# Short GpSimd memsets between the gathers of a two-layer graph network

## The chip, the cores and the metric

The kernel runs on one core of a Trainium2 chip. The core has five engines that work side by side[...]: PE (matrix products), DVE (vector work), ACT (activations), POOL (GpSimd, which here mostly issues gathers) and SP (which here only issues DMAs). The metric is the device time of one execution in microseconds (us), as the median of several executions.

## The reference

There are N = 6250 nodes with 256 features and 200,000 edges with 128 attributes. The edges are sorted by their destination `dst`; their sources `src` are random. Two layers follow one another, each with a residual and a layer norm.

```python
# layer 1: messages over the edges, added up by destination
e = edge_attr @ W_edge + b_edge
msg = relu(x[src] + e)
agg = segment_sum(msg, dst)
h = (1 + eps) * x + agg
h = relu(h @ W1 + b1) @ W2 + b2
h = relu(batchnorm_over_nodes(h) * gamma + beta)
x = layernorm(x + h)
# layer 2: attention with 4 heads of 64
z = einsum('nd,hdf->nhf', x, W)
e = leaky_relu(es[src] + ed[dst])      # es, ed: products of z with att
alpha = softmax of e over the edges of one destination
out = segment_sum(alpha * z[src], dst)
x = layernorm(x + out)
```

Both layers read one row of a table for each edge at random: `x[src]` in the first, `z[src]` in the second. Those are the gathers that this case is about.

## The kernel before

**Tiles.** The edges are cut into 1563 subtiles of 128 edges (one edge to a partition), and 14 subtiles make a group (`S = 14`), so there are 112 groups, the last with 9 subtiles. Since the edges are sorted, the destinations of a group lie in a window of at most 128 neighbouring nodes, and one-hot matrices on PE do the segment sums.

**Layer 1** (`edge_messages`) works through pairs of subtiles. For pair k:

- `fetch` (L537, gathers at L542) issues on POOL one indirect DMA for each subtile, which reads 128 rows of 256 floats by the ids in a column of `src_sb` into half of a tile `XG[k]`. The pool of these tiles holds 14 pairs, so POOL can be up to 28 gathers ahead of their use. The first 20 groups read the input x, later ones a table `xb_tab` with the bias added in.
- `features` (L546) computes the edge term on PE into PSUM.
- `sums` (L554, L556) adds the gathered rows on DVE; with this the tile `XG[k]` comes free.
- `upper` (ACT, L561) and `lower` (DVE, L565) take the relu as the sum of a high and a low part, and `add_up` (PE, L575) adds both up by destination into an accumulator of the group.

When a group ends, `flush` (L454) corrects the accumulator, runs the two dense layers of the window and keeps statistics for the batch norm.

**The middle** (`middle`, L677) takes the batch norm, layer norm and the tables of layer 2; POOL adds the residual there (L727).

**Layer 2** works by groups. `gather` (L877, gathers at L883) issues on POOL 14 gathers of 264 floats from `z_tab` into a ring of 4 groups. DVE computes the weights and multiplies the rows by them (`weigh`, y at L1007), PE adds them up (L1011), and `leave` finishes the rows of a group (`finish_steps`: fin at L369, the layer norm's root by way of L322 and L325) and sends them out.

**What sets the order.** The bodies of both layers stand in a block which fixes the order of four engines as written:

```python
with tc.manual_schedule(engines={ET.DVE, ET.PE, ET.Activation, ET.SP}):
```

POOL is not among them. Its instructions are put in order by the scheduler of the language, which keeps what data and buffers demand and is otherwise free to choose. The same holds in layer 2 (L1047).

Of the kernel before, what the change touches and what calls it, by code (L numbers as in the profile page):

```python
# [6 lines left out]
F32 = mybir.dt.float32  # L7
# [25 lines left out]
XB_FROM = 20  # L33
RING = 4
XTB = 4
FIRST = 256
IN_RANGE = "the value is an id of a node, which the kinds of inputs bound"

# [10 lines left out]
def gnn(ctx, tc, io, N, E):  # L49
    nc = tc.nc  # L50
# [10 lines left out]
    def groups(g):  # L61
        return range(gs[g], gs[g + 1])
# [4 lines left out]
    const = ctx.enter_context(tc.tile_pool(name="const", bufs=1))  # L67
# [40 lines left out]
    nc.vector.memset(nil, 0.0)  # L108
    ones3 = const.tile([3, P], BF16, name="ones3")
    nc.vector.memset(ones3, 1.0)  # L110


    gf = const.tile([P, 2 * G], F32, name="gf")
# [325 lines left out]
    with ExitStack() as st:  # L439
# [97 lines left out]
        def fetch(k):  # L537
            g, j0, w = pairs_[k]
            XG[k] = gp.tile([P, 2, D], F32, tag="xg", name="xg")
            for i in range(w):  # L540
                t = gs[g] + j0 + i
                nc.gpsimd.indirect_dma_start(  # L542
                    out=XG[k][:, i, :], out_offset=None, in_=io["x"] if g < GB else xb_tab,
                    in_offset=bass.IndirectOffsetOnAxis(ap=src_sb[:, t:t + 1], axis=0))

        def features(k):  # L546
            g, j0, w = pairs_[k]
            pt = PT[k] = pe.tile([P, 2, D], F32, tag="pe", name="pt")
            for i in range(w):
                if g < GB:  # L550
                    nc.tensor.matmul(pt[:, i, :], ones3, bias3, start=True, stop=False)
                nc.tensor.matmul(pt[:, i, :], EA.pop(gs[g] + j0 + i), we_sb, start=not g < GB, stop=True)  # L552
# [35 lines left out]
        with tc.manual_schedule(engines={ET.DVE, ET.PE, ET.Activation, ET.SP}):  # L588
# [16 lines left out]
            for f in (0, 1):  # L605
                if f < K:
                    fetch(f)
                    features(f)
# [8 lines left out]
            for k in range(K + 2):  # L617
# [10 lines left out]
                j = k - firsts_[g] if k < K else 99  # L628
                if k + 2 < K:
                    fetch(k + 2)  # L630
                    features(k + 2)
# [45 lines left out]
    def middle(h2T, stats):  # L677

        with ExitStack() as st:
# [28 lines left out]
            nc.sync.dma_start(ed_tab[NB * P:], zero[:, 0, :EW])  # L708
            cuts = [0] + [min(c0, NB * P) for c0 in range(FIRST, NB * P + CH, CH)]
            cs = list(zip(cuts, cuts[1:]))  # L710
            M = {}

            def load(ci):
                c0, c1 = cs[ci]
                xt = yp.tile([P, 2, CH], F32, tag="xt", name="xt", bufs=XTB)
                nc.sync.dma_start(xt[:, :, :c1 - c0], io["xT"].rearrange("(k p) n -> p k n", p=P)[:, :, c0:c1])
                M["xt", ci] = xt
# [75 lines left out]
            none = iter(())  # L793
            for ci in range(min(XTB - 1, nch)):
                load(ci)
            with tc.manual_schedule(engines={ET.DVE, ET.PE, ET.Activation, ET.SP}):
                for i in range(nch + 3):
                    if i + XTB - 1 < nch:
                        load(i + XTB - 1)
                    a, b, d = (f(j) if 0 <= j < nch else none  # L800
# [45 lines left out]
    with ExitStack() as st:  # L846
# [20 lines left out]
        def size(g):  # L867
            return gs[g + 1] - gs[g]
# [8 lines left out]
        def gather(g):  # L877
            n = size(g)
            slot = T["slot"] if T["slot"] + n <= RING * S else 0
            T["slot"] = slot + n  # L880
            zg = ring[:, slot:slot + n]
            for j, t in enumerate(groups(g)):
                nc.gpsimd.indirect_dma_start(  # L883
                    out=zg[:, j, :], out_offset=None, in_=z_tab,
                    in_offset=bass.IndirectOffsetOnAxis(ap=src_sb[:, t:t + 1], axis=0))
            T["zg", g] = zg

        def loads(g):
# [157 lines left out]

        with tc.manual_schedule(engines={ET.DVE, ET.PE, ET.Activation, ET.SP}):  # L1047
            gather(0)
            loads(0)
            loads(min(1, G - 1))  # L1050
# [4 lines left out]
            for i in range(G + 2):  # L1055
# [3 lines left out]
                if i + 1 < G:  # L1059
                    gather(i + 1)  # L1060
# [253 lines left out]
```

## Time and profile before

| what | value |
|---|---|
| median of 3 runs | 5119.02 us (5110.36 to 5121.45) |
| the profiled execution's own time | 5185.35 us |
| its span on the core | 5183.5 us |
| layer 1's gathers (L542) | 1563, some 0.95 us busy each |
| layer 2's gathers (L883) | 1563, 0.960 us busy each |
| POOL busy | 3014.6 us, 58% of the span |
| mean granted clock of PE | 0.775 |

Layer 1 takes roughly the first 2560 us, the middle some 125 us, and layer 2 runs from about 2685 to 5110 us, with a tail to the end of the span.

How to read it: the profile gives for each engine the busy time and the number of instructions. In a row of a group, the name after the line and engine is what the instruction writes and, after the arrow, reads; behind the bar stand its total busy time, the mean of one in ns, and the time that the engine idled just before such instructions with what ended the idling (the releaser). "issue" as a releaser means that nothing which the profile shows was waited for, and "remote" that the wait ended by an event that the profile can't put down to one of the instructions. A row of waits reads: engine and line that waited, what it waited for, us in total, times, and the longest. A row of windows gives a stretch, its length, busy time and number of the chosen instructions, and then granted clock, DMA share and GB/s.

### The profile page before, as it was taken

What the parts mean: (1) busy time and instruction counts of PE and PEld (TensorE: products, weight loads), DVE (VectorE), ACT (ScalarE), POOL (GpSimd) and SP (SyncE); (2) the same over time, 40 slices, a digit from 0 to 9 for tenths busy, and PEclk for the clock granted to TensorE, in tenths of its full rate; (3) what the DMA queues carried; (4) which work ended last, traced back from release to release, by engine and by line L of the source; (5) the groups of instructions that cost most, each with busy time, mean ns of one, the idle gap of its engine ahead of it and who ended that gap; (6) DMA issues with size and microseconds to landing.
All of it is one profiled execution on the core that took longest, in us unless ns stands there. A gap on an engine that the chain in (4) does not pass through costs nothing. (4 is left out here: it accounts for less than half of the span.)

```text
span 5183.5 us, 49111 instructions
## 1 busy us (share of the span) xinstructions
PE 3157.2 (61%) x12883; PEld 2163.7 (42%) x12883; DVE 3178.2 (61%) x8203; ACT 1055.2 (20%) x3046; POOL 3014.6 (58%) x3158
## 2 busy tenths in 40 slices
PE   6888666556666666666653655655555655555555
PEld 3455454444545445544542333333333333333333
DVE  4665656555565556655664666666666666666666
ACT  2222222222222222222340111111111111111111
POOL 5565565555555555555446666666666666656662
PEclk9898888888887888888876677666667667767667
DMA  4644443333444443434373444444444444444442
GB/s 157 212 133 132 141 133 115 125 106 127 130 132 130 130 134 125 123 127 132 95 198 107 126 116 126 125 124 118 117 120 122 122 120 120 124 119 120 119 115 70
DMA packets 298029, 656.24 MB, mean 127 GB/s; under 512 B 86827, under 2 KB 170139, under 8 KB 290572
## 3 DMA queue, kind: packets, MB, share of 16 engines
q0 software_dynamic: 150144, 416.54, 29.4%
q1 hardware_dynamic: 146090, 235.43, 13.4%
q8 instruction: 106, 1.74, 0.1%
q14 instruction: 183, 1.50, 0.1%
q10 hardware_dynamic: 1506, 1.04, 0.1%
HBM read 617.82 MB, written 34.99 MB: 126 GB/s over the span
## 5 line engine op out<-in xcount | busy, mean ns | idle before, releaser
L883 POOL DMA_INDIRECT ring<-z_tab,src_sb x1563 | 1500.6, 960 | 944.9 <-DVE frs L325 377.8
L1011 PE MATMUL acc<-y,oh 128*128 128x260 f32 x3126 | 1178.6, 521 | 1013.6 <-DVE y L1007 914.9
L542 POOL DMA_INDIRECT xg<-xb_tab,src_sb x1283 | 1213.1, 946 | 886.7 <-DVE pt L556 537.9
L552 PE MATMUL pt<-we_sb,ea_t 128*128 128x256 f32 x3126 | 1036.4, 453 | 477.6 <-DVE hl L565 410.6
L1011 PEld LDWEIGHTS acc<-y,oh 128*128 128x128 f32 x3126 | 722.7, 252 | 1307.3 <-DVE y L1007 1061.5
L552 PEld LDWEIGHTS pt<-we_sb,ea_t 128*128 128x128 f32 x3126 | 626.3, 222 | 675.1 <-issue 463.4
L556 DVE TENSOR_TENSOR pt<-pt,xg 128x512 f32<-128x512 f32 x782 | 540.9, 692 | 432.6 <-PE acc L575 168.2
L575 PE MATMUL acc<-hl,oh 128*128 128x512 f32 x1563 | 721.8, 546 | 1.1 <-DVE hl L565 1.1
L561 ACT ACTIVATE hl<-pt 128x512 fp32r<-128x512 f32 x782 | 466.3, 597 | 1096.0 <-DVE pt L556 634.3
L1007 DVE TENSOR_TENSOR y<-ring,cst 128x520 f32<-128x520 f32 x782 | 528.4, 676 | 77.9 <-remote 57.9
L565 DVE SCALAR_TENSOR_TENSOR hl<-pt,hl 128x512 fp32r<-128x512 f32 x782 | 532.0, 680 | 2.0 <-ACT hl L561 2.0
L369 DVE SCALAR_TENSOR_TENSOR fin<-rows,edw,fin 128x256 f32<-128x256 f32 x112 | 54.0, 482 | 671.0 <-remote 661.4
L542 POOL DMA_INDIRECT xg<-in_x,src_sb x280 | 266.4, 951 | 191.6 <-DVE pt L556 115.0
L575 PEld LDWEIGHTS acc<-hl,oh 128*128 128x128 f32 x1563 | 341.1, 218 | 62.4 <-DVE hl L565 1.9
L414 DVE SCALAR_TENSOR_TENSOR pmk<-p,mk 128x128 f32<-128x128 f32 x224 | 56.3, 289 | 474.2 <-ACT h2T L404 456.5
L400 PE MATMUL p<-r,w_sb 128*128 128x128 f32 x896 | 152.3, 323 | 256.5 <-ACT r L395 169.7
L400 PEld LDWEIGHTS p<-r,w_sb 128*128 128x128 f32 x896 | 133.3, 225 | 294.8 <-ACT r L395 188.0
L523 DVE TENSOR_TENSOR oh<-iota_p,dloc 128x896 fp32r<-128x896 f32 x224 | 241.3, 1078 | 0.0
L322 ACT ACTIVATE frs<-fmv,eps_c 128x1 f32<-128x1 f32 x112 | 33.0, 295 | 1020.5 <-DVE fmv L373 910.4
L933 DVE TENSOR_TENSOR oh<-cst,dloc 128x896 f32<-128x896 f32 x224 | 239.5, 1069 | 0.2 <-ACT cst L993 0.2
L1023 ACT COPY ag<-acc 128x260 f32<-128x260 f32 x111 | 41.6, 375 | 616.7 <-issue 359.6
L395 ACT ACTIVATE r<-p,cols 128x128 f32<-128x128 f32 x224 | 69.8, 364 | 380.2 <-remote 290.2
(219 smaller groups left out, 2940.9 us busy)
## 6 DMA issues: line engine op xcount, KB each, us to landing
ea_t<-in_eaT SPq DMA_DIRECT2D x54, 1792.0 KB
dlb<-dl_tab SPq DMA_DIRECT2D x111, 448.0 KB
ring<-z_tab,src_sb POOLq DMA_INDIRECT x1563
xg<-xb_tab,src_sb POOLq DMA_INDIRECT x1283
xw<-in_x SPq DMA_DIRECT2D x112, 128.0 KB
hw<-hT_tab SPq DMA_DIRECT2D x112, 128.0 KB
out<-o SPq DMA_DIRECT2D x110, 128.0 KB
xr<-in_x SPq DMA_DIRECT2D x24, 256.0 KB
```

The source lines that it names most:

```text
L400: nc.tensor.matmul(p2[:, m, :], w2_sb[:, k, m * P:(m + 1) * P], r1[:, k, :], start=(k == 0), stop=(k == 1))
L523: nc.vector.tensor_tensor(OH[g][:, c0:c1], iota_p.unsqueeze(1).to_broadcast([P, c1 - c0, P]), dl.unsqueeze(2).to_broadcast([P, c1 - c0, P] ...
L542: nc.gpsimd.indirect_dma_start(out=XG[k][:, i, :], out_offset=None, in_=io["x"] if g < GB else xb_tab, in_offset=bass.IndirectOffsetOnAxis ...
L552: nc.tensor.matmul(pt[:, i, :], EA.pop(gs[g] + j0 + i), we_sb, start=not g < GB, stop=True)
L556: nc.vector.tensor_add(PT[k][:, :w], PT[k][:, :w], XG.pop(k)[:, :w])
L561: nc.scalar.activation(HL[k][:, :w, 0], PT[k][:, :w], AF.Relu)
L565: nc.vector.scalar_tensor_tensor(HL[k][:, :w, 1], PT.pop(k)[:, :w], 0.0, HL[k][:, :w, 0].bitcast(F32), op0=OP.max, op1=OP.subtract)
L575: nc.tensor.matmul(ACC[g].rearrange("p a d -> p (a d)"), OH[g][:, j0 + i], hl[:, i].rearrange("p a d -> p (a d)"), start=(j0 + i == 0), st ...
L883: nc.gpsimd.indirect_dma_start(out=zg[:, j, :], out_offset=None, in_=z_tab, in_offset=bass.IndirectOffsetOnAxis(ap=src_sb[:, t:t + 1], axi ...
L933: nc.vector.tensor_tensor(T["oh", g][:, c0:c1], iota_p.unsqueeze(1).to_broadcast([P, c1 - c0, P]), dloc[:, gs[g] + c0:gs[g] + c1].unsqueez ...
L1007: nc.vector.tensor_tensor(y[:, :w], T["zg", g][:, j0:j0 + w, :ZW].rearrange("p s (h f) -> p s h f", f=F + 1), by_edge(T["ex", g], g)[:, j0 ...
L1011: nc.tensor.matmul(T["acc", g].rearrange("p h f -> p (h f)"), T["oh", g][:, j0 + i, :], y[:, i].rearrange("p h f -> p (h f)"), start=(j0 + ...
```

## The change

A tile of one partition with 768 floats is set up, and a function that clears it on GpSimd. In layer 1 it is called after gathers 6 and 13 of a group, in layer 2 after gathers 4, 9 and 13 (counted from 0).

```diff
+RESTS1 = (6, 13)
+RESTS2 = (4, 9, 13)
...
+    rest_t = const.tile([1, 768], F32, name="rest_t")
+
+    def breathe():
+
+        nc.gpsimd.memset(rest_t, 0.0)
...
                 nc.gpsimd.indirect_dma_start(
                     out=XG[k][:, i, :], out_offset=None, in_=io["x"] if g < GB else xb_tab,
                     in_offset=bass.IndirectOffsetOnAxis(ap=src_sb[:, t:t + 1], axis=0))
+                if j0 + i in RESTS1:
+                    breathe()
...
                 nc.gpsimd.indirect_dma_start(
                     out=zg[:, j, :], out_offset=None, in_=z_tab,
                     in_offset=bass.IndirectOffsetOnAxis(ap=src_sb[:, t:t + 1], axis=0))
+                if j in RESTS2:
+                    breathe()
```

Nothing reads `rest_t`. In the changed file the memset stands in line 118, layer 1's gathers in line 550 and layer 2's in line 893.

## The prediction

> **What bounds the kernel now.** I read the page's head, then its groups by line, the chain of waits, then windows and the timeline around GpSimd's gathers. No engine is full over the span: the busiest, DVE and PE, stand at 61%, GpSimd at 58%.
>
> ```profile
> span 5183.5 us, 49111 instructions
> PE 3157.2 (61%) x12883; PEld 2163.7 (42%) x12883; DVE 3178.2 (61%) x8203; ACT 1055.2 (20%) x3046; POOL 3014.6 (58%) x3158
> L883 POOL DMA_INDIRECT ring<-z_tab,src_sb x1563 | 1500.6, 960 | 944.9 <-DVE frs L325 377.8
> L542 POOL DMA_INDIRECT xg<-xb_tab,src_sb x1283 | 1213.1, 946 | 886.7 <-DVE pt L556 537.9
> L542 POOL DMA_INDIRECT xg<-in_x,src_sb x280 | 266.4, 951 | 191.6 <-DVE pt L556 115.0
> ```
>
> Nearly all of POOL is its 2 x 1563 gathers. In layer 1 they run up to 28 ahead of the sums that use them (14 pair buffers) and then wait for DVE's sum L556 to free one. The timeline shows the two kinds of step, the free one and the one that waits (the first column is the start, the second the duration, the bracket the idle time before it):
>
> ```profile
> 706.01 0.95 POOL L542 DMA_INDIRECT xg<-xb_tab,src_sb  x1 [0.30 <-issue]
> 707.26 0.95 POOL L542 DMA_INDIRECT xg<-xb_tab,src_sb  x1 [0.30 <-issue]
> 711.58 0.94 POOL L542 DMA_INDIRECT xg<-xb_tab,src_sb  x1 [3.38 <-DVE pt L556]
> ```
>
> A free gather takes 707.26 - 706.01 = 1.25 us from start to start, 14 of a group 17.5 us. The group itself lasts longer: the waits of the window from 3 to 951 us say by how much POOL is early.
>
> ```profile
> POOL xg L542 <- DVE pt L556: 244.1, 92, 6.8
> POOL xg L542 <- issue: 127.8, 408, 0.9
> ```
>
> So POOL is not the bound of layer 1, but it has little to give.[...] by the row's 946 ns the first 580 gathers are 549 us of work and POOL is free for 400 us of the first 951; by start to start they are 580 x 1.251 = 725.6 us and it is free for 951.1 - 3 - 725.6 = 222 us. I use the second, since the 0.30 us between gathers appears even where nothing is waited for.
>
> **Where the change really lands.** GpSimd is not among the engines whose order is written out by hand, so the scheduler places its instructions. A memset on `rest_t` depends on nothing but the memset before it, while a gather waits for a buffer. In the built program the 557 memsets (224 written in layer 1, 333 in layer 2: 111 groups x 5, and the last group of 9 gathers has 2) therefore do not stand after gathers 6 and 13, or 4, 9 and 13, of each group. All 557 stand before or among the first 580 gathers of layer 1, in batches of 1 to 8, mostly after every second gather:
>
> ```
> after gather   70  140  210  280  350  420  490  560  580
> memsets so far 36  143  208  267  339  401  459  536  557
> ```
>
> None comes after gather 580, in group 41 of 112, and none in layer 2. PE, DVE, ACT and SP keep their instruction orders. Nothing is removed and no DMA is added; the DMAs of the first 580 gathers start later, behind the memsets on POOL, and no other queue is passed.
>
> **Cost of one memset.** No 1x768 memset is in the trace. The nearest POOL rows:
>
> ```profile
> L727 POOL TENSOR_TENSOR hn<-hn,xt 128x512 f32<-128x512 f32 x22 | 28.9, 1322 | 27.7 <-ACT hn L725 17.9 <-DVE rr L331 9.7
> L727 POOL TENSOR_TENSOR hn<-hn,xt 128x256 f32<-128x256 f32 x2 | 1.4, 719 | 43.6 <-ACT hn L725 43.6
> L1301 POOL MEMSET const-float32-0.0<- 128x1 f32 x1 | 0.1, 99 | 0.2 <-issue 0.2
> ```
>
> Below: the memset of one element, 0.10 us. Above: the two-input operation's slope, (1322 - 719) / 256 = 2.36 ns an element, gives 719 + 512 x 2.36 = 1.93 us at 768. That it has one partition and not 128 may help, but no row shows it. [...]0.80 us, an estimate.[...]I leave the sums at their 692 ns.
>
> **The sum.** POOL's way to gather 580: 3 (its first gather starts there) + 725.6 + 557 x 0.80 = 445.6, together 1174 us; each of the 234 batches also parts two gathers, at 0 to 0.30 us each (the gap that already stands before every gather), and I take 0.1: 23 us. That makes 1197 us, with no waiting on DVE at all. Before, these stood so:
>
> ```profile
> 0.00:951.10 951.10, 550.26 (x580) 0.86 0.46 145
> 0.00:999.10 999.10, 200.76 (x290) 0.86 0.45 144
> ```
>
> The first line is POOL L542 up to gather 580, the second DVE L556 up to the sum of that pair: POOL was 48 us ahead of it. Of the 469 us added, then, 222 take the place of POOL's idle time, and another 48 less 3.5 eat the lead (3.5 us is from a gather's start to the first work behind it: 4018.34 - 4014.79 in the fence below). What is left is on the path: 1197 + 3.5 - 999 = +201 us. The cover is per group, about 22.8 - 17.5 = 5.3 us, against 557 / 41 = 13.6 memsets a group, 11 us with their gaps. In groups 5 to 41 the group will take 17.5 + 11 = 28 to 29 us, and DVE, PE and ACT wait for the gathered rows.
>
> **After gather 580** POOL has no lead. It streams free until it is 28 gathers ahead again, 35 us. In such unbroken streams the results of PE reach the other engines late; layer 2 shows it in each group:
>
> ```profile
> DVE fin L369 <- remote: 661.4, 95, 9.0
> 4014.79 0.95 POOL L883 DMA_INDIRECT ring<-z_tab,src_sb  x1 [0.30 <-issue]
> 4018.34 0.48 DVE L369 SCALAR_TENSOR_TENSOR fin<-rows,edw,fin 128x256 f32<-128x256 f32 x1 [7.44 <-remote]
> 4020.35 0.94 POOL L883 DMA_INDIRECT ring<-z_tab,src_sb  x1 [4.62 <-DVE frs L325]
> ```
>
> DVE sits idle for 7.44 us and goes on only when the run of gathers has ended. If the rebuild holds the sums completely, the whole 35 us are lost; if not at all, none. I take 15. The rest of layer 1, the middle and layer 2 stay as they are, because no memset stands there: this is 0, covered by nothing and needing no cover.
>
> Sum: +201 + 15 = **+216 us**, of the profiled execution's 5185.35 us: 5401. That execution lies 1.3% above the median of the runs shown, so for those 5119 + 216 = **5335 us**.
>
> How the price moves it: each 0.1 us of a memset is 55.7 us. At 0.60 us the time is 5224, at 1.10 us 5502. The change breaks even where 557 p + 23 equals the 222 + 44.5 us of slack and lead, so p = 0.44 us.
>
> **Rivals.**
> - *The memset is short and vanishes in POOL's idle time* (the other side). Under 0.44 us a memset everything lies in the 222 us of waits on L556 and in the lead. The breaks in the stream may then let PE's results through sooner: at most the "remote" waits of that window, 66.8 us for L556 and 61.4 us for ACT's r. Half of half of these gives 5119 - 32 = 5087; with no such gain 5119. For it: one partition is written, and the 99 ns row. Against: 768 elements along the row[...].
> - *The dear memset*[...]
> - *The change does what the source says*: two rests in a group of layer 1, three in layer 2, 1.6 and 2.4 us against the 5.3 us, and 21.7 - 17.5 = 4.2 us, of POOL's waits in a group. Hidden, 5119; if a rest let DVE's 7.44 us pass, several hundred us faster. Against: the order in the built program is fixed, and has none there.
>
> **How the numbers follow.** The likeliest case (price 0.60 to 1.10 us) 0.80; between 0.44 and 0.60, 5135 to 5224 us, 0.06; short memset 0.05; dear 0.07; order as written 0.02. The range takes the likeliest case with the rebuild's 0 to 35 us: 5225 to 5505. 0.2%, 10 us, is about what a measurement of this kernel tells from no change. Faster: 0.03 of the short memset, 0.01 of the order as written. Same: the rest of these two, 0.03. Slower 0.93.
>
> **What would show it.** In the changed kernel's profile: L118 POOL MEMSET x557, all before about 1.2 ms, starts 0.8 us apart inside a batch; POOL without waits on DVE L556 from 100 us to 1.2 ms, and DVE L556 waiting for POOL or its gathers there; gather 580 at about 1197 us; the first waits of POOL on L556 some 35 to 100 us later; layer 2's stretch of about 2425 us unchanged, with L369's remote wait still near 660 us. Wrong would be: memsets that start under 0.44 us apart (no loss), over 1.1 us (more loss), memsets found in layer 2 (another order), or a DVE L556 that goes on waiting for PE where it should wait for gathers (then the end isn't set by POOL).

## The result

The changed kernel takes 5289.78 us (median of 4 runs, 5263.56 to 5297.23), the kernel before 5120.24 us (median of 4, 5110.36 to 5138.41): a ratio of 1.0318, 95% interval 1.0272 to 1.0364, so about 170 us slower. The forecast was 5335 us with a range from 5225 to 5505.

The profiled execution of the changed kernel took 5263.56 us, the lowest of its four, while that of before (5185.35) lies above its runs. The two pages are thus only 78 us apart; a second pair, taken on one chip (below), is 153 us apart and is shown beside it.

One thing has to be known to read the numbers of the experiments: they ran on several chips, and the same kernel before takes 5109 to 5203 us on some of them (call these long chips) and 4107 to 4125 us on others (short chips); each comparison is with before on its own chip. The runs are called e1 to e12: e1 to e4, e7, e8, e11 and e12 met short chips, e5, e6, e9 and e10 long ones.

**The memsets.** From the page of the changed kernel, its head and POOL's groups:

```profile
span 5261.8 us, 49668 instructions
PE 3227.3 (61%) x12883; PEld 2195.1 (42%) x12883; DVE 3209.2 (61%) x8203; ACT 1052.3 (20%) x3046; POOL 3416.8 (65%) x3715
L893 POOL DMA_INDIRECT ring<-z_tab,src_sb x1563 | 1496.2, 957 | 913.5 <-issue 346.5
L550 POOL DMA_INDIRECT xg<-xb_tab,src_sb x1283 | 1214.5, 947 | 693.3 <-DVE pt L566 345.8
L118 POOL MEMSET rest_t<- 1x768 f32 x557 | 405.3, 728 | 19.0 <-POOLq L1313 0.3
L550 POOL DMA_INDIRECT xg<-in_x,src_sb x280 | 267.6, 956 | 73.4 <-issue 67.5
```

POOL has gained 557 instructions and 402 us of busy time, and a memset takes 0.728 us. Before the 280 gathers from x POOL had waited 115.0 us for DVE's sums; that releaser has dropped out of the row. Where the memsets stand is told by the view of their tile, whose row has the shortest, median and longest duration in ns and the first and last start:

```profile
L118 POOL MEMSET rest_t<- x557: 727/727/777, 0.8 to 1127.9; 1x768 f32 x186
```

All are over by 1128.6 us, in layer 1, also the 334 that are written in layer 2. The timeline of POOL shows what one costs:

```profile
707.53 0.95 POOL L550 DMA_INDIRECT xg<-xb_tab,src_sb  x1 [0.16 <-issue]
708.78 0.94 POOL L550 DMA_INDIRECT xg<-xb_tab,src_sb  x1 [0.31 <-issue]
709.72 0.73 POOL L118 MEMSET rest_t<- 1x768 f32 x1
710.61 0.95 POOL L550 DMA_INDIRECT xg<-xb_tab,src_sb  x1 [0.16 <-issue]
...
714.96 0.94 POOL L550 DMA_INDIRECT xg<-xb_tab,src_sb  x1 [0.30 <-issue]
715.89 2.30 POOL L118 MEMSET rest_t<- 1x768 f32 x3
718.36 0.95 POOL L550 DMA_INDIRECT xg<-xb_tab,src_sb  x1 [0.17 <-issue]
```

The memset at 709.72 us starts at once when the gather ends (708.78 + 0.94), and the next gather follows it after 0.16 us and not 0.30. From gather to gather one memset makes 710.61 - 708.78 = 1.83 us of 1.25 (+0.58), three make 718.36 - 714.96 = 3.40 (+2.15). So memsets that follow one another start (2.15 - 0.58) / 2 = 0.785 us apart, and each batch (the memsets between two gathers) saves 0.785 - 0.58 = 0.205 us of the gap. The expectations below use 0.775 and 0.19, which comes to nearly the same sum: 387 and not 389 us for the 557.

**POOL has become the bound there.** The waits of the changed kernel from 100 to 1128 us:

```profile
DVE pt L566 <- DMA xg<-xb_tab,src_sb: 217.4, 107, 8.1
DVE pt L566 <- DMA xg<-in_x,src_sb: 134.7, 61, 8.4
POOL xg L550 <- DVE pt L566: 1.1, 6, 0.3
```

POOL waits for DVE's sums 1.1 us in all, and DVE's sums wait 352 us for gathered rows: the relation of before is turned round. Groups 3 to 41 of layer 1, which start at 62.7 and end at 1138.8 us, now take 27.6 us each by the starts of their gathers; before it was 23.3 us.

**After the memsets** POOL streams on until it is ahead again. DVE's sums in the timeline of the changed kernel:

```profile
1132.97 0.70 DVE L566 TENSOR_TENSOR pt<-pt,xg 128x512 f32<-128x512 f32 x1 [0.27 <-DMA xg<-xb_tab,src_sb]
...
1157.39 0.70 DVE L566 TENSOR_TENSOR pt<-pt,xg 128x512 f32<-128x512 f32 x1 [13.10 <-remote]
1173.48 0.70 DVE L566 TENSOR_TENSOR pt<-pt,xg 128x512 f32<-128x512 f32 x1 [14.80 <-remote]
1184.77 0.48 DVE L464 SCALAR_TENSOR_TENSOR ag<-xw,opem,acc 128x256 f32<-128x256 f32 x1 [10.00 <-remote]
```

Two sums wait 13.10 and 14.80 us while the stream runs, and a step of `flush` 10.00 us. At 1186.59 POOL meets its first long wait on L566 again:

```profile
1177.51 0.95 POOL L550 DMA_INDIRECT xg<-xb_tab,src_sb  x1 [0.30 <-issue]
1186.59 0.94 POOL L550 DMA_INDIRECT xg<-xb_tab,src_sb  x1 [8.13 <-DVE pt L566]
```

Where the time went, by the starts of single instructions in the four traces (us; e5 and e6 below are before and the changed kernel on one chip):

| | before | changed | more | before, e5 | changed, e6 | more |
|---|---|---|---|---|---|---|
| gather 580 | 951 | 1129 | 178 | 961 | 1131 | 170 |
| its sum on DVE | 999 | 1133 | 134 | 1010 | 1136 | 126 |
| sum of gather 700 | 1219 | 1361 | 142 | 1230 | 1373 | 143 |
| last sum of layer 1 | 2583 | 2697 | 114 | 2583 | 2739 | 156 |
| first gather of layer 2 | 2685 | 2799 | 114 | 2686 | 2841 | 155 |
| last gather of layer 2 | 5109 | 5188 | 79 | 5119 | 5272 | 153 |
| span | 5184 | 5262 | 78 | 5193 | 5346 | 153 |

In both pairs the loss is made before gather 700. What the first pair gives back after that has no instruction of the change in it; in the pair of one chip it isn't there. The medians differ by 170 and, on one chip, 151 us; the traces place 142 and 143 us of these, and what makes the rest is not shown.

### The profile page after: what moved, and what is told of

It is laid out like the page before. It is cut to its first block, busy times and chain, and to the rows that moved or that the text cites. A ratio compares the mean times of both kernels' runs of the same rounds, so it can differ in the third digit from the quotient of the medians.

```text
span 5261.8 us, 49668 instructions
## 1 busy us (share of the span) xinstructions
PE 3227.3 (61%) x12883; PEld 2195.1 (42%) x12883; DVE 3209.2 (61%) x8203; ACT 1052.3 (20%) x3046; POOL 3416.8 (65%) x3715
## 5 line engine op out<-in xcount | busy, mean ns | idle before, releaser
L1023 PE MATMUL acc<-y,oh 128*128 128x260 f32 x3126 | 1203.6, 530 | 979.9 <-DVE y L1019 821.5
L562 PE MATMUL pt<-we_sb,ea_t 128*128 128x256 f32 x3126 | 1055.8, 460 | 590.0 <-DVE hl L575 510.3
L1023 PEld LDWEIGHTS acc<-y,oh 128*128 128x128 f32 x3126 | 733.6, 256 | 1283.2 <-DVE y L1019 967.9
L566 DVE TENSOR_TENSOR pt<-pt,xg 128x512 f32<-128x512 f32 x782 | 542.7, 694 | 651.4 <-DMA xg<-xb_tab,src_sb 219.5
L585 PE MATMUL acc<-hl,oh 128*128 128x512 f32 x1563 | 737.1, 557 | 1.1 <-DVE hl L575 1.1
L118 POOL MEMSET rest_t<- 1x768 f32 x557 | 405.3, 728 | 19.0 <-POOLq L1313 0.3
L377 DVE SCALAR_TENSOR_TENSOR fin<-rows,edw,fin 128x256 f32<-128x256 f32 x112 | 54.1, 483 | 566.9 <-remote 541.6
```

The lines of the kernel that those rows point to most:

```text
L118: nc.gpsimd.memset(rest_t, 0.0)
L566: nc.vector.tensor_add(PT[k][:, :w], PT[k][:, :w], XG.pop(k)[:, :w])
L585: nc.tensor.matmul(ACC[g].rearrange("p a d -> p (a d)"), OH[g][:, j0 + i], hl[:, i].rearrange("p a d -> p (a d)"), start=(j0 + i == 0), st ...
L1023: nc.tensor.matmul(T["acc", g].rearrange("p h f -> p (h f)"), T["oh", g][:, j0 + i, :], y[:, i].rearrange("p h f -> p (h f)"), start=(j0 + ...
```

## The experiments

POOL's order can be fixed too, if it is added to the two blocks that write out the order of both layers; this is the tool of most runs:

```diff
-        with tc.manual_schedule(engines={ET.DVE, ET.PE, ET.Activation, ET.SP}):
+        with tc.manual_schedule(engines={ET.DVE, ET.PE, ET.Activation, ET.SP, ET.Pool}):
```

Without memsets this alone gives the very program of before, instruction for instruction, and in the traces of e7 to e10 every engine's other instructions stand in the order of before, but for one or two neighbouring pairs on DVE at the setting up of tiles. So what these runs show comes from the memsets.

### Before and the changed kernel on one chip

e5 and e6 are the two kernels without an edit.

> The kernel before, unchanged, for its profile beside these runs, in which it took 4118.6 us and not 5120. Theory: here POOL is the bound. 3126 gathers x 1.251 = 3911 us, with the middle (about 125) and the tail (about 70) 4106 us; then POOL's waits on L556 and the remote waits of L369 (653 and 661 us in the profile of before) are nearly gone. Rival: only a faster PE clock, with the same waits scaled by about 0.8.

> The changed kernel, unchanged. If before takes about 4119 us beside it, POOL is the bound throughout: 557 x 0.775 - 234 x 0.19 = +387 us less what POOL waited before gather 580 (20 to 40 us), so +350 to +370, about 4480 us. If before takes about 5120 us beside it, POOL's waits cover over half: +135 to +175, about 5275 us. Rival: the loss is the same in us in both.

Measured: before 5192.65 us (5182.94 to 5203.41), the changed kernel 5343.69 us, ratio 1.0284 (1.0254 to 1.0315), +151 us. This chip took 5193 us where the four runs before it had been on one with 4119, so the theory about those is not tested by e5. The waits of e5 are those of before:

```profile
DVE fin L369 <- remote: 697.0, 100, 10.3
POOL xg L542 <- DVE pt L556: 653.5, 213, 8.6
```

The +151 us lie in the expected +135 to +175: of the memsets' 389 us of POOL time more than half is covered by POOL's waits. The changed kernel met no short chip, so the rival of e6, the same loss on both kinds, is not tested by it. In e6 the L377 wait (L369 of before) is 679.9 us, and layer 2 from its first to its last gather is 2431 us against 2432: layer 2 hasn't changed.

### The rests of layer 2 alone

```diff
-RESTS1 = (6, 13)
+RESTS1 = ()
```

> Only the rests written in layer 2 (334), none in layer 1, and POOL's order left to the scheduler: all of them stand before gather 347 of layer 1. Theory: the loss is in layer 1: POOL reaches gather 346 after 3 + 346 x 1.251 + 334 x 0.775 - 137 x 0.19 = 669 us, against a sum of that pair at about 617 us before: +52 and up to 35 for the lead, 5170 to 5210 us; layer 2's stretch does not change. Rival (they act in layer 2): layer 1's stretch is as before, and all of the difference lies after 2685 us.

Measured: 4321.35 us against 4118.6, ratio 1.0497 (1.0479 to 1.0514), +203 us. The tile's row tells where these rests of layer 2 ran:

```profile
L118 POOL MEMSET rest_t<- x334: 727/727/734, 0.8 to 675.1; 1x768 f32 x167
```

All in layer 1, done by 676 us where 669 was worked out. So the rival falls. The expected +52 to +87 us was not met, because it was for a chip with POOL's waits; on this one there is little to hide in: 334 x 0.785 - 137 x 0.205 = 234 us, of which 203 are paid.

### The same places, shorter memsets

The order of the changed kernel was written out by hand (`HOIST` holds the 234 batches, such as 3 before gather 0, 3 before gather 14) and POOL's order fixed, so that only the length differs: 8 or 384 floats.

```diff
+                for _ in range(HOIST.get(t, 0)):
+                    breathe()
                 nc.gpsimd.indirect_dma_start(
...
-    rest_t = const.tile([1, 768], F32, name="rest_t")
+    rest_t = const.tile([1, 8], F32, name="rest_t")
```

> The 557 memsets stand exactly where the changed kernel has them (order of POOL fixed by hand at those places), but clear 8 floats and not 768. Theory (the loss is POOL time in layer 1): about 0.1 us each, 557 x 0.1 = 56 us less the gaps that they replace, all of it in the 222 us of POOL's waits: 5119 us within 15. Rival (what counts is that another instruction parts the gathers, or the order): still about +170, 5290 us.

> As the one with 8 floats, but 384. If the time of a memset is 0.08 us plus 0.85 ns a float, one takes 0.41 us, in a batch 0.45: 557 x 0.45 - 234 x 0.19 = 206 us of POOL, below its 222 us of waits before gather 580. Theory (break-even near 0.44 us): 5119 us within 30, so far less than half of the 170 us that 768 floats cost. Rival (a loss in proportion to the length): +85, 5205 us.

Measured beside a before of 4118.6 us: 4215.9 us with 8 floats (1.0245, 1.0228 to 1.0262, +97 us) and 4327.81 with 384 (1.0512, 1.0495 to 1.0530, +209 us). Both expectations missed: as in e4, POOL has next to no waits here to hide a memset in. In e2 its waits for DVE's sums are no longer than the gap that stands before a gather anyway, or than that behind a batch:

```profile
POOL xg L566 <- DVE pt L580: 54.3, 151, 0.6
```

The two serve as price instead: where POOL is the bound, 384 floats cost 209 us where 206 was worked out. The tile's rows of the two, first 8 floats, then 384:

```profile
L132 POOL MEMSET rest_t<- x557: 94/94/507, 0.8 to 860.9; 1x8 f32 x186
```

```profile
L132 POOL MEMSET rest_t<- x557: 407/408/424, 0.8 to 974.7; 1x384 f32 x186
```

With a median of 727 ns at 768, a float costs (727 - 408) / 384 = 0.83 ns and the instruction about 0.09 us besides, where 0.85 and 0.08 had been assumed.

The kernel with 8 floats was run again on another chip:

> 557 memsets of 8 floats at the changed kernel's places. Beside a before of about 5190 us: theory, 557 x 0.17 = 97 us of POOL (as measured where POOL was the bound) stay below its 222 us of waits before gather 580: within 20 us of before. Rival (the presence or the order of the memsets, not their time): +100 to +150 us, like the changed kernel's +151. Beside a before of about 4115 us: +97 us.

Measured: 5074.95 us against 5133.2 (5109.08 to 5145.88), ratio 0.9889 (0.9848 to 0.9929), 58 us faster. The theory that the time of the memsets makes the loss holds, and the rival, that their presence or order does, falls: 557 memsets at the same places lose nothing when they are short. They even gain, and by more than the 20 us that the theory allowed. In the trace of e10 gather 580 starts at 906 us, against 951 and 961 in the two of before, so a good part of the gain seems to be made where the memsets stand. How much is not shown: no trace of before was taken on e10's chip, where before takes 50 to 60 us less than in those two.

### The rests where the source writes them

Only POOL's order is fixed, and the rests stay where the change writes them. Three runs, on three chips:

> The same memsets, but POOL's order is fixed as written too, so they stand after gathers 6 and 13 of each group of layer 1 and after 4, 9 and 13 of each group of layer 2. A rest adds 0.58 us to the stream (0.73 us of memset, and the gap before the next gather falls from 0.30 to 0.16). Theory A, POOL's waits cover it (5.3 and 4.2 us a group against 1.2 and 1.7 us): 5119 us within 20. Theory B, a rest lets PE's late results through: layer 2's 661 us of remote waits at L369 fall by over half, 4700 to 5000 us. Theory C, the late results only come when a run of gathers has ended, and each run is now longer: 112 x (1.16 + 1.74) = +325, about 5440 us.

> The rests where the source writes them, once more, now hoped for beside a before of about 5190 us. Theory A, POOL's waits of 4 to 5 us a group cover 1.16 and 1.74 us: within 20 us of before. Theory B, a rest of 0.73 us lets PE's late results through: remote waits of L369 fall by half or more and the time by 200 us or more. Theory C, the late results come only when a run of gathers has ended and the run is longer by the rests: up to +325 us. Beside a before of about 4120 us POOL is the bound and +329 us is expected again.

> The rests where the source writes them, for a comparison beside a before of about 5190 us. Theory A, POOL's waits of 4 to 5 us a group cover 1.16 and 1.74 us: within 20 us of before. Theory B, a rest lets PE's late results through: 200 us or more faster. Theory C, the late results come only when a run of gathers has ended, and the run is longer: up to +325 us. Beside a before of about 4115 us: +330 us, as measured twice.

| run | before, us | with rests as written, us | ratio | 95% interval |
|---|---|---|---|---|
| e1 | 4118.6 | 4447.43 | 1.0807 | 1.0789 to 1.0825 |
| e7 | 4113.34 | 4443.65 | 1.0809 | 1.0790 to 1.0827 |
| e9 | 5133.2 | 4913.03 | 0.9566 | 0.9528 to 0.9603 |

The same kernel is 8.1% slower on two chips and 4.3% faster on a third. On the first two the loss is the POOL time to within 7 us: 557 x 0.58 = 323, measured 329 and 330. The waits of e7 show that POOL has next to none there (200 waits of 0.39 us on average, where 0.30 us is the usual gap):

```profile
POOL xg L550 <- DVE pt L566: 78.9, 200, 3.3
POOL ring L893 <- DVE frs L333: 2.7, 9, 0.3
```

In e9 the outcome is that of theory B. The waits of that kernel, to be held against those of before (652.9 us for xg, 661.4 for fin and 377.8 for ring), though the traces of before come from other executions, 5185 and 5195 us long:

```profile
POOL xg L550 <- DVE pt L566: 372.4, 169, 9.2
DVE fin L377 <- remote: 302.3, 50, 20.4
POOL ring L893 <- DVE frs L333: 80.7, 29, 4.1
```

The remote wait of a group's last rows has fallen from 95 times to 50 and by more than half, and the finished rows hold POOL up less (DVE frs: 377.8 to 80.7 us).

The way in which these waits end has changed too. In the trace of before, 80 of the 95 remote waits end while POOL stands still, 2.3 to 2.9 us after the end of its last gather; in e5 it is 86 of 100 and in e10 78 of 92, but in e9 none of 50, and half of these end while POOL goes on. So the waits that last until a run of gathers is over are the ones that are gone.

It is not all of the gain. Layer 2, from first to last gather, takes 2307 us against 2425 and 2432 before, and it starts at 2549 us against 2685 and 2686: about half of the gain is made before layer 2, where there are two rests a group. There the account is mixed: POOL's waits on the sums and ACT's remote wait at r (290.2 to 65.9 us) fell, but a remote wait that the trace of before does not have came up:

```profile
DVE ag L464 <- remote: 187.2, 51, 5.2
```

Over all engines and lines the remote waits fell from 1473 to 1175 us. What the rests of each layer are worth alone, in their places on a long chip, was not run.

The timeline of POOL in e9 has a pause of 0.89 us between the end of one gather and the start of the next:

```profile
3907.00 0.95 POOL L893 DMA_INDIRECT ring<-z_tab,src_sb  x1 [0.30 <-issue]
3907.94 0.73 POOL L118 MEMSET rest_t<- 1x768 f32 x1
3908.83 0.95 POOL L893 DMA_INDIRECT ring<-z_tab,src_sb  x1 [0.16 <-issue]
```

and in DVE's timeline of e9, in the same stretch, one group passes without a remote wait and the next still meets it:

```profile
3905.50 0.48 DVE L377 SCALAR_TENSOR_TENSOR fin<-rows,edw,fin 128x256 f32<-128x256 f32 x1 [1.39 <-PE acc L1023]
3928.52 0.48 DVE L377 SCALAR_TENSOR_TENSOR fin<-rows,edw,fin 128x256 f32<-128x256 f32 x1 [7.90 <-remote]
```

So on this long chip three rests a group in layer 2 and two in layer 1, in their places, cost 323 us of POOL and return more, 220 us net; in layer 2, which is 118 to 125 us shorter, L377's remote waits are 302.3 us against 661.4 of L369 before. This version beats before there, and loses to it on the short chips. The changed kernel itself was run on none of these chips.

### Shorter, and one long rest

The rests as written with 8 floats, and one rest of four memsets in layer 2 alone (the diff is of the second; POOL's order is fixed in both):

```diff
-RESTS1 = (6, 13)
-RESTS2 = (4, 9, 13)
+RESTS1 = ()
+RESTS2 = (5,)
...
-        nc.gpsimd.memset(rest_t, 0.0)
+        for _ in range(4):
+            nc.gpsimd.memset(rest_t, 0.0)
```

> The rests where the source writes them, POOL's order fixed, but 8 floats long: the stream is parted by some 0.15 us and not 0.58. Beside a before of 5110 to 5200 us: if the length of the pause lets PE's late results through, little of the 4.3% gain of 768 floats is left (ratio 0.985 to 1.005); if any instruction between the gathers does it, the gain is the same or larger (0.94 to 0.96). Beside a before of about 4115 us: +557 x 0.15, about +85 us.

> No rest in layer 1; in layer 2 one rest a group, of four memsets (4 x 0.775 = 3.1 us, 2.95 us of stream), after gather 5, where DVE begins to wait at L369; POOL's order fixed as written. Beside a before of about 5190 us: if a pause of 3 us lets the late results through, L369's 7.4 us become about 3.5 us, and with 14 x 1.251 + 2.95 = 20.5 us of stream a group of 22.0 us falls to 20.5 at best: -100 to -170 us. If it doesn't, the run is 2.95 us longer: up to +330 us. Beside a before of about 4120 us: 112 x 2.95 = +330 us.

> In layer 2 alone one rest of four memsets a group, after gather 5 (2.95 us of stream). Beside a before of 5110 to 5200 us: if one long pause lets the late results through better than three short ones, layer 2 takes 20.5 us a group and the kernel is over 2% faster; if what counts is how often the stream is parted, it gains less than 1% or loses. Beside a before of about 4115 us: +337 us, as measured.

All three met short chips, with a before of 4113.34 and 4113.98 us, so what length of pause lets the results through, and whether one long pause does it, was not found out. Measured: 8 floats 4123.8 us, ratio 1.0023 (1.0016 to 1.0031), only +10 us and not +85; the long rest 4450.34 us (1.0827, 1.0806 to 1.0848) and 4449.23 (1.0826, 1.0802 to 1.0850), +336 us on average where +330 and +337 were expected. Why 8 floats are free when alone is in e11's timeline of POOL:

```profile
1003.40 0.95 POOL L550 DMA_INDIRECT xg<-xb_tab,src_sb  x1 [0.30 <-issue]
1004.34 0.09 POOL L118 MEMSET rest_t<- 1x8 f32 x1
1004.66 0.95 POOL L550 DMA_INDIRECT xg<-xb_tab,src_sb  x1 [0.22 <-DVE hl L575]
```

The memset stands inside the 0.30 us that lie between two gathers anyway: 1.26 us from start to start instead of 1.25. At the changed kernel's places, 2.4 to a batch, the same 557 had cost 97 us. There the gap behind a batch of two or more is 0.61 us, as in e2's timeline:

```profile
506.52 0.94 POOL L566 DMA_INDIRECT xg<-xb_tab,src_sb  x1 [0.30 <-issue]
507.46 0.24 POOL L132 MEMSET rest_t<- 1x8 f32 x2
508.32 0.95 POOL L566 DMA_INDIRECT xg<-xb_tab,src_sb  x1 [0.61 <-DVE hl L589]
```

Two memsets of 8 floats thus part two gathers by 508.32 - 506.52 = 1.80 us, nearly as much as one of 768 (1.83). So the gain of e10, which has the same batches, doesn't tell whether a shorter pause would do.

## Why the prediction was right

**The place: right.** All 557 memsets ran before or among the first 580 gathers of layer 1, the last at 1127.9 us, and layer 2 stayed as it was (2431 against 2432 us in the pair of one chip; in the first pair it was 36 us shorter). Of them 223 are written in layer 1 and 334 in layer 2; the prediction has 224 and 333, a slip in the split that doesn't touch the sum.

**The price: right, a little high.** 0.80 us was taken, 0.785 measured from start to start (0.728 of duration and 0.057 to the start of the next). The 0.80, like its bounds of 0.60 and 1.10, was the author's estimate between two far ends: no row of before shows it. Both ends were far off the 0.728 measured, the memset of one element with 0.10 us and the slope of the two-input row with 1.93; that slope is 2.36 ns an element, while a float of the memset took 0.83. A dearer memset than 1.10 us had no row of before behind it either, and did not come. DVE's sums, left at 692 ns, took 697 before gather 580: nothing in the sum.

**The gap of a batch: mis-sized, with the wrong sign.** The prediction added 0.1 us for each of 234 batches, 23 us. The memset does not add a gap, it takes part of the one that was there: -0.205 us a batch, -48. With 557 x 0.785 = 437 us, POOL's way to gather 580 is 3 + 725.6 + 437 - 48 = 1118 us where 1197 was predicted and 1129 measured. Of the 11 us left, 8 are five gaps of 1.9 us and not 0.3, with no memset in them, before gathers 113, 219, 325, 431 and 537, each 106 after the last; before has none there, and their cause is open:

```profile
216.97 0.95 POOL L550 DMA_INDIRECT xg<-in_x,src_sb  x1 [1.93 <-issue]
434.17 0.94 POOL L550 DMA_INDIRECT xg<-in_x,src_sb  x1 [1.93 <-issue]
```

The gap of a batch, mis-sized by 71 us, makes nearly all of the difference between the predicted +201 us at that sum and the measured +134 and +126.

**The cover: right.** POOL's 222 us of waits and its lead of 48 us are used up: POOL's waits on L566 fell to 1.1 us, and gather 580 was 178 us later in the one pair while its sum was only 134 us later, and 170 and 126 in the other: 44 us of lead, where 48 less 3.5 was predicted. The groups take 27.6 us; 28 to 29 was predicted.

**The lead rebuilt: in the range, the figure a guess.** 15 us was taken between 0 and 35 without a reason for the middle. Between gathers 580 and 700 the delay of the sums grows from 134 to 142 us in the first pair and from 126 to 143 in the other, so by 8 and 17 us. The long remote waits lie there in both traces. But "goes on only when the run of gathers has ended" is too strong for this stretch: the sums at 1157.39 and 1173.48 us started while gathers still ran, up to 1178 us. In layer 2 it fits most groups, and not "each": L369 waits so in 95 of 112. That POOL would meet its sums again 35 to 100 us after gather 580 is borne out: 1186.59 - 1128.75 = 58 us.

**The rest as nothing: right** in the pair of one chip, 153 us at the end against 143 at gather 700. L377's remote wait is 542 us in the changed kernel's own profile, not near 660, but 680 in e6 against 697 in e5: that row differs by more from one execution to another than by the change.

**The range** is narrower than its own terms. With a price of 0.60 us and no rebuild the sum is 5209 us, with 1.10 us and all 35 us of it 5523; the text has 5225 and 5505. The total of +216 came out 46 us above the measured +170. Against the 142 and 143 us that the traces place it is 73 us too high, nearly all by the gap of a batch; the 27 us between are luck.

**The rival that the change does what the source says** did not happen as built, and there it was right to give it little. What the prediction says of its worth was borne out by e9: with the order fixed the rests gain 220 us, and L377's remote wait falls by more than half. But its cover, "POOL's waits of a group", isn't there in every run: where before takes 4115 us, the same rests cost 330 us.

## What to carry to other kernels

With this scheduler an instruction that depends on nothing stays where it is written only if its engine's order is fixed; elsewhere look for it in the built program, since here 334 instructions of layer 2 ran in the first 37% of layer 1's gathers. Price small instructions on GpSimd by start to start, in the neighbourhood where they will stand: here one of 8 floats lay in the 0.30 us that stand between two gathers anyway (1.26 us from start to start, not 1.25), and two didn't (1.80 us). Before an engine's idle time is spent, ask where the idle time comes from, and whether every chip shows it: here the same rests gained 4.3% beside a before of 5133.2 us and lost 8.1% beside 4118.6 and 4113.34.

## What the runs showed of the hardware

**Two kinds of chip.** The kernel before takes 4113 to 4119 us (medians) on three chips of these runs and 5120 to 5193 us on the others, a ratio of 1.25, while the runs of before beside one comparison agree within 1%. In the profiles of e2, e7 and e11, from short chips, the waits have no remote row at all, and the 3126 gathers of 1.251 us, 3911 us, nearly fill the kernel (4121.1 us in e11). No trace of before was taken on a short chip. PE's mean granted clock is 0.82 to 0.84 in those and 0.76 to 0.78 in the profiles from long chips; 0.84 / 0.76 = 1.11, against 1.25 in the times: if the time went with the clock alone, the clocks would not make up the difference. Each chip was met on one occasion, so chip and occasion aren't told apart.

**Late results.** In the trace of before all 95 "remote" waits of L369 end at an update of PE's own semaphore, and in that of the changed kernel all 87 of L377. The update comes 6.2 us (median of the 95; 6.0 of the 87) after the end of the last instruction of PE that could have given it, though the profile only models these ends.

**What is open.** What makes the results late on one chip and not on another: no run here takes the cause itself away. The length of pause that is needed. And whether the 384 floats at the changed kernel's places, 206 us of POOL, would have vanished in the 222 us of waits on a long chip.
